# A graph transformer on one core: a pick of rows serves eight batches instead of four

## The chip, the core and the metric

The kernel runs on one core of a Trainium2 chip. The core has a matrix engine (TensorE, PE in the profile; its weight loads are listed apart as PEld), a vector engine (VectorE, DVE), a scalar engine (ScalarE, ACT), a general engine (GpSimd, POOL), which here only issues indirect gathers, and SyncE (SP), which only issues transfers. Each works through its own list of instructions in order and waits for the others through semaphores. The metric is the time on the device of one execution, in microseconds (us), the median of several runs.

## The reference

Three layers of a graph transformer run over 6,250 nodes with 64 features and 206,250 edges, sorted by target node; then a log-softmax, a residual and a normalization. One layer, shortened:

```python
q = x @ Wq + bq
k = x @ Wk + bk
v = x @ Wv + bv
e = edge_attr @ We
kj = k[src] + e
alpha = jnp.sum(q[dst] * kj, axis=-1) / jnp.sqrt(jnp.float32(D))
amax = jax.ops.segment_max(alpha, dst, num_segments=N)
p = jnp.exp(alpha - amax[dst])
denom = jax.ops.segment_sum(p, dst, num_segments=N)
w = p / denom[dst]
msg = (v[src] + e) * w[:, None]
agg = jax.ops.segment_sum(msg, dst, num_segments=N)
return agg + x @ Ws + bs
```

What matters here is `x[src]`: every edge needs the 64 features of its source node, and the sources are random.

## The kernel before

**Batches and steps.** The edges lie in 403 chunks of 512, four chunks to a batch (`LB`), so 100 full batches and a remainder. A layer runs over the batches in 99 steps (variable `u`) and some steps written out at its end. The nodes are 49 blocks of 128.

**Picked and gathered rows.** In layer 0 every chunk from batch 8 (`U0`) on is sorted on the chip by source: 22 windows (`WINDOWS`) of 16 slots (`SL`), where window w holds edges whose source lies in blocks 2w to 2w+3. Rows of edges with a slot need no gather. They are *picked*: for a pair of windows q, a one-hot matrix says which node of a block each slot wants (`hot`, built on VectorE from the `key` of each slot, in `aim`), and TensorE multiplies node rows (`halves`, split in three bf16 parts so that their sum is exact) by it: four blocks, three parts, two windows, 24 products (L1374 in `bank`). ScalarE copies the result from the accumulator `ps_x` into a ring, `kept` (L1383, L1386). Layer 0 has 8 such pairs, layers 1 and 2 have 11 (`PAIRS`). Edges without a slot are fetched by indirect DMA on GpSimd (L601), in layers 1 and 2 five transfers a batch, each let go by a small copy on ScalarE (`gate`, L635).

**Turns.** One pick serves four batches (`TURN`): 4 batches x 4 chunks x 16 slots = 256 columns. The pair q is picked at batches k with q % 4 = k % 4, so that in layers 1 and 2 three, three, three and two picks fall to successive steps, 283 picks a layer counting those cut at the layer's ends. The ring `kept` holds four batches. At step u the picks due at u+2 are made; by then step u has turned batch u+1 from the ring into rows (`naturals`).

**A step of layers 1 and 2** is, on TensorE: the scores of the last unit (L1673, L1678), the turning of the next batch from the ring (L1399, L1404), one pick (the *first place*), a transpose of gathered rows (L1650), the transposes of the probabilities (L1704), the other picks that are due (the *second place*), and the sums (L1717). VectorE reduces the scores (L1685), ScalarE takes the exponentials (L1692) and VectorE copies the transposed probabilities (L1707) in between. Work on finished groups of nodes (`finish`, `project`) is spread over the steps (`close_up`). There are two sets of four one-hot tiles; the next set is built as soon as a pick has been issued, in the buffers of that pick.

**Keys.** In layer 0 the `index` function of the sort writes each batch's keys to DRAM (`keyS`), in an order in which a pick's four batches lie side by side, in one or two transfers from ScalarE's queue; `load` reads a pick's keys with one transfer on SP that repeats them on all 128 partitions (L1307). Up to 7 key tiles wait in layers 1 and 2, and 3 in layer 0.

**The sort in layer 0.** `ranking` counts, for a set of chunks, the edges of each bin, one bin after the other. For each: a product of TensorE, a ScalarE pass that adds the carried count (`order`, L932), and a one-column VectorE operation that takes the new carried count `served` (L935) from its result, then a pause (`yield`) and two VectorE passes (L939, L940). `Move.across` turns sorted features and stores them through one buffer, `eN` (L1104).

**Boundaries.** Step 0 of layers 1 and 2 needs all eleven pairs picked for the first batches; this is done as far as possible while the last node groups of the layer before are finished (`early`), and the rest after them.

Of the kernel before, what the change touches and what calls it, by code (L numbers as in the profile page):

```python
# [39 lines left out]
KEYED = 12  # L40
PART = SLOTS - 2 * P
REST = P - PART
TURN = 4
GC = 16
# [398 lines left out]
def main_path(  # L443
# [80 lines left out]
    picks = ctx.enter_context(tc.tile_pool(name="picks", bufs=3))  # L524
# [8 lines left out]
    sorts = first_layer.enter_context(tc.tile_pool(name="sorts", bufs=2))  # L533

# [18 lines left out]
    keyS = dram.tile([KEYED, NT // TURN + 1, TURN, LB, 2 * SL], FP16, name="keyS")  # L553
# [317 lines left out]
    kept = {0: const.tile([P, TURN * LB, P], F32, name="kept0")}  # L871
    keys = const.tile([LB, KEYED, 2 * SL], FP16, name="keys")
# [20 lines left out]
    def ranking(i):  # L893
# [31 lines left out]
        for h in range(WINDOWS + 1):  # L925
# [7 lines left out]
            if h < WINDOWS:  # L933
                kinds = kinds_of(h + 1)
            nc.vector.tensor_scalar(  # L935
                served[:n, h + 1 : h + 2], order[:, CH - 1 :], float(SL * min(h + 1, WINDOWS) - 1), None, ALU.min
            )
            yield
# [72 lines left out]
    class Move:  # L1011
# [86 lines left out]
        def across(self, i):  # L1098
# [4 lines left out]
            eN = sorts.tile([P, 2 * T * D], F32, name="eN", bufs=1)  # L1103
# [5 lines left out]
        def index(self):  # L1109
# [16 lines left out]
            key = keys  # L1126
            order = key.rearrange("c (b a) (w e) -> c w a b e", b=TURN, w=2)
            for w in range(2):
                nc.vector.tensor_copy(
                    order[:, w, : FULL // TURN],  # L1130
                    pk[:, w * P : (w + 1) * P].rearrange("c (a b e) -> c a b e", b=TURN, e=SL),
                )
            tail = pk[:, 2 * P :].rearrange("c (h e) -> c h e", e=SL)
            nc.scalar.copy(order[:, :, 2, 2], tail[:, 2:4])
            for w in range(2):
                nc.scalar.copy(order[:, w, 2, :2], tail[:, 4 * w : 4 * w + 2])  # L1136
# [143 lines left out]
    class Picker:  # L1280


        def __init__(self, layer):
            self.layer = layer
            low = 0 if layer else U0
            self.jobs = []
            for k in range(low - TURN + 1, NT):
                for q in range(PAIRS[layer]):
                    if q % TURN == k % TURN:
                        self.jobs.append((k, max(k, low), min(k + TURN, NT), q))  # L1290
            self.loads, self.aims = list(self.jobs), list(self.jobs)
            self.keys, self.hots = {}, {}
            self.aimed = 0

        def load(self):

            while self.loads and len(self.keys) < (7 if self.layer else 3):
# [3 lines left out]
                shape = [P, TURN * LB * 2 * SL]  # L1301
                if self.layer:
                    key = later.tile(shape, FP16, name="key", bufs=7)
                else:
                    key = picks.tile(shape, FP16, name="key", bufs=3)
                a, b = self.span(job)
                nc.sync.dma_start(  # L1307
                    key[:, a * 2 * SL : b * 2 * SL],
                    keyS[q % TURN * KEYED // TURN + q // TURN, (job[0] + TURN) // TURN, a // LB : b // LB].rearrange("r c e -> (r c e)").partition_broadcast(P),
                )  # L1310
# [3 lines left out]
        def span(self, job):  # L1314

            _, k0, k1, _ = job
            return (0, TURN * LB) if k1 - k0 == TURN else (k0 % TURN * LB, ((k1 - 1) % TURN + 1) * LB)

        def aim(self):
# [23 lines left out]
        def due(self, k):  # L1343

            if not self.jobs or self.jobs[0][0] > k:
                return False
# [9 lines left out]
        def bank(self, k, tag="x"):  # L1356
# [7 lines left out]
            made = self.hots.pop(job)  # L1364
            q = job[3]
# [702 lines left out]
```

## Time and profile before

| what | value |
|---|---|
| median of three runs | 4270.91 us (4266.38 to 4275.15) |
| the profiled execution, its own time | 4275.86 us |
| the profiled execution, first to last instruction (span) | 4274.1 us |
| granted TensorE clock, mean | 0.948 |
| layer 0, steps | to about 1935 us |
| layer 1, steps | about 2056 to 3060 us |
| layer 2, steps | about 3180 to 4190 us |

The profile is one execution as the hardware recorded it. A row of a view gives source line, engine, operation, what is written and read (`out<-in`), the shape, a count, the busy time, the mean time of one in ns, and the engine's idle time just before such instructions with what ended it. Records of neighbouring products overlap, so the time a product costs is read from the starts of groups. "issue" means that the engine waited for nothing that the profile shows. The line numbers are those of the kernel before.

### The profile page before, as it was taken

What the parts mean: (1) busy time and instruction counts of PE and PEld (TensorE: products, weight loads), DVE (VectorE), ACT (ScalarE), POOL (GpSimd) and SP (SyncE); (2) the same over time, 40 slices, a digit from 0 to 9 for tenths busy, and PEclk for the clock granted to TensorE, in tenths of its full rate; (3) what the DMA queues carried; (4) which work ended last, traced back from release to release, by engine and by line L of the source; (5) the groups of instructions that cost most, each with busy time, mean ns of one, the idle gap of its engine ahead of it and who ended that gap; (6) DMA issues with size and microseconds to landing.
All of it is one profiled execution on the core that took longest, in us unless ns stands there. A gap on an engine that the chain in (4) does not pass through costs nothing.

```text
span 4274.1 us, 125157 instructions
## 1 busy us (share of the span) xinstructions
PE 3681.7 (86%) x44542; PEld 2464.7 (58%) x44542; DVE 2891.1 (68%) x9241; ACT 2394.9 (56%) x7113; POOL 2067.3 (48%) x1910
## 2 busy tenths in 40 slices
PE   4679998889999999987889999998778998888885
PEld 2345555555555655654666666666456666666663
DVE  5566888787788777774566666666456666666664
ACT  2334555555555555543566666666536676666664
POOL 4454554555455665552444444444415444444442
PEclk9789999999999999997999999999879999999997
DMA  5447787787777888874677777777647777777773
GB/s 119 101 131 188 201 213 203 192 211 200 206 198 211 226 212 209 218 196 131 146 183 189 192 185 186 188 193 182 152 96 191 177 181 184 187 186 179 176 187 83
DMA packets 828647, 768.02 MB, mean 180 GB/s; under 512 B 393233, under 2 KB 628903, under 8 KB 828014
## 3 DMA queue, kind: packets, MB, share of 16 engines
q1 hardware_dynamic: 673282, 571.05, 54.2%
q10 hardware_dynamic: 93932, 126.48, 8.4%
q0 software_dynamic: 60800, 62.38, 7.8%
q8 instruction: 356, 5.83, 0.6%
q14 instruction: 277, 2.27, 0.2%
HBM read 599.30 MB, written 160.27 MB: 178 GB/s over the span
## 4 chain that ended last, share of the span: by engine, by line


## 5 line engine op out<-in xcount | busy, mean ns | idle before, releaser
L601 POOL DMA_INDIRECT feat<-in_x,gate x860 | 1050.6, 1222 | 884.4 <-ACT gate L635 686.4
L1331 DVE TENSOR_SCALAR hot<-key,rank 128x512 bf16<-128x512 f16 (+3 forms) x3024 | 908.2, 350 | 372.5 <-PE ps_x L1374 167.5
L601 POOL DMA_INDIRECT feat<-x,gate x816 | 796.8, 976 | 745.3 <-ACT gate L635 479.1
L1374 PEld LDWEIGHTS <-halves 128*64 128x64 bf16 x18144 | 963.4, 113 | 285.7 <-issue 206.1
L1374 PE MATMUL ps_x<-hot,halves 128*64 128x256 bf16 (+1 forms) x13248 | 836.7, 276 | 41.6 <-issue 31.2
L1717 PE MATMUL ps_g<-feat,probT 128*32 128x128 f32 x9672 | 436.5, 283 | 92.4 <-issue 61.6
L1064 PE MATMUL ps_x<-hit,rest 128*64 128x512 bf16 (+3 forms) x3200 | 459.1, 359 | 6.0 <-issue 5.1
L1409 ACT COPY featT<-kept 64x512 f32<-64x512 f32 x584 | 361.5, 619 | 144.3 <-PE ps_g L1374 42.6
L1053 DVE TENSOR_SCALAR hit<-ruler,pos 128x512 bf16<-128x512 f16 (+3 forms) x1600 | 422.9, 334 | 1.7 <-PE ps_m L1078 1.4
L1717 PEld LDWEIGHTS ps_g<-feat,probT 128*32 128x32 f32 x9672 | 286.5, 112 | 221.5 <-issue 175.6
L1685 DVE TENSOR_REDUCE most<-ps_s 128x1 f32<-128x512 f32 x297 | 204.1, 687 | 300.6 <-PE ps_s L1678 111.9
L601 POOL DMA_INDIRECT few<-x,gate x198 | 193.6, 978 | 379.4 <-ACT gate L635 113.0
L1374 PE MATMUL ps_g<-hot,halves 128*64 128x256 bf16 (+2 forms) x4560 | 302.3, 281 | 74.1 <-ACT kept L1383 28.5
L1653 ACT COPY featT<-ps_a 64x512 f32<-64x512 f32 x584 | 338.6, 580 | 15.6 <-PE ps_a L1650 4.1
L1678 PE MATMUL ps_s<-featT,q 128*32 128x512 f32 x2376 | 333.7, 621 | 2.9 <-ACT featT L1653 1.3
L1064 PE MATMUL ps_x<-hit,raw 128*64 128x512 bf16 (+3 forms) x1600 | 311.0, 367 | 4.5 <-issue 4.1
L1383 ACT COPY kept<-ps_x 128x256 f32<-128x256 f32 (+2 forms) x502 | 185.1, 370 | 210.8 <-remote 128.6
L635 ACT COPY gate<-src_b 128x1 int32<-128x1 int32 x1762 | 289.9, 191 | 8.7 <-ACT keys L1136 1.4
L1692 ACT ACTIVATE prob<-ps_s,part 128x512 f32<-128x512 f32 x297 | 204.2, 688 | 161.0 <-issue 48.7
L1704 PE MATMUL ps_p<-ident,prob 128*128 128x128 f32 (+1 forms) x1224 | 199.1, 286 | 91.9 <-ACT prob L1692 89.8
L1064 PEld LDWEIGHTS <-rest 128*64 128x64 bf16 x3200 | 203.8, 113 | 116.6 <-issue 30.0
L1725 ACT COPY part<-ps_g 128x128 f32<-128x128 f32 (+1 forms) x309 | 82.2, 266 | 273.0 <-PE ps_g L1717 43.8
(261 smaller groups left out, 5162.4 us busy)
## 6 DMA issues: line engine op xcount, KB each, us to landing
feat<-eaP SPq DMA_DIRECT2D x292, 512.0 KB
featT<-eaS SPq DMA_DIRECT2D x292, 512.0 KB
key<-keyS SPq DMA_DIRECT2D x712, 128.0 KB
raw<-in_ea SPq DMA_DIRECT2D x200, 256.0 KB
eaS<-eT ACTq DMA_DIRECT2D x200, 256.0 KB
eaP<-eN ACTq DMA_DIRECT2D x200, 256.0 KB
to<-toS SPq DMA_DIRECT2D x292, 128.0 KB
part<-part SPq DMA_DIRECT2D x600, 32.5 KB
```

Of the source, the lines that this page charges most:

```text
L601: nc.gpsimd.indirect_dma_start(out=spares[layer, k] if c is None else loaded[layer, k][:, c, t, 0], out_offset=None, in_=xts[layer][:, :], ...
L635: copy(gate, index[:, i : i + 1])
L1053: nc.vector.tensor_scalar(hit, ruler[:, : REACH[t]], self.pos[:, at : at + 1], None, ALU.is_equal)
L1064: nc.tensor.matmul(self.px[i][j * D : (j + 1) * D, : REACH[t]], self.part(i, part)[:, (j * T + t) * D : (j * T + t + 1) * D], self.hits[t, ...
L1331: nc.vector.tensor_scalar(hot[:, a:b].rearrange("p k w e -> p (k w e)"), self.keys[job][:, a * 2 * SL : b * 2 * SL], rank[:, h : h + 1], None,
L1374: nc.tensor.matmul(px[w * D : (w + 1) * D, a:b], third(halves[block >= EARLY][:, at : at + 1], part)[:, 0], made[h][:, a:b, w], start=(h = ...
L1409: nc.scalar.copy(featT[:D, :, w * P : (w + 1) * P], kept[0][w * D : (w + 1) * D, at : at + LB])
L1653: nc.scalar.copy(self.featT[:D, :, at : at + P], pt[h * D : (h + 1) * D])
L1678: nc.tensor.matmul(self.p_s[rows], self.q[:, j * STRIDE : j * STRIDE + W], self.featT[:, j, :], start=False, stop=True)
L1685: nc.vector.tensor_reduce(top[:n], self.p_s[:n], AX.X, ALU.max)
L1692: nc.scalar.activation(self.prob[:n], self.p_s[:n], AF.Exp, bias=self.part[:n, P : P + 1], accum_out=self.part[:n, P + 1 : P + 2],)
L1717: nc.tensor.matmul(p_g[rows, :].rearrange("n (h d) -> n h d", h=2), self.probT[:, t, rows], batch[:, c + j, t], start=(t == 0), stop=(t == ...
```

## The change

One pick of layers 1 and 2 serves eight batches: 512 columns to a product, and the pair q is picked at batches with q % 8 = k % 8. Pairs 0 and 8, 1 and 9, 2 and 10 fall together, so successive steps have 2, 2, 2, 1, 1, 1, 1, 1 picks, 148 a layer. Where one pick is due its 24 products are divided: the first 12 in the first place (`open`), the others and the copy in the second (`shut`). The ring holds eight batches in layers 1 and 2; the one of layer 0 is a tile of its own. Both sets of one-hots stand in one pool, with two times four tiles of twice the size; 5 key tiles of twice the size take the place of 7. Layer 0 keeps turns of four.

The keys in DRAM are ordered by pair and batch. A batch's keys are written with one transfer; a pick whose first batch isn't at the start of the ring reads its keys with two. In the sort, the carried count `served` is taken after the pause, and `across` has two buffers.

```diff
 TURN = 4
+TURNS = (TURN, 8, 8)
...
-    keyS = dram.tile([KEYED, NT // TURN + 1, TURN, LB, 2 * SL], FP16, name="keyS")
+    keyS = dram.tile([WINDOWS // 2, NT, LB, 2 * SL], FP16, name="keyS")
...
             if h < WINDOWS:
                 kinds = kinds_of(h + 1)
+            yield
             nc.vector.tensor_scalar(
                 served[:n, h + 1 : h + 2], order[:, CH - 1 :], float(SL * min(h + 1, WINDOWS) - 1), None, ALU.min
             )
-            yield
...
-            eN = sorts.tile([P, 2 * T * D], F32, name="eN", bufs=1)
+            eN = sorts.tile([P, 2 * T * D], F32, name="natural", bufs=2)
...
-            r = k % TURN
-            for phases, job in ((slice(0, r + 1), k // TURN + 1), (slice(r + 1, TURN), k // TURN)):
-                if phases.start < phases.stop:
-                    those = slice(phases.start * KEYED // TURN, phases.stop * KEYED // TURN)
-                    nc.scalar.dma_start(keyS[those, job, r].rearrange("q c e -> c q e"), key[:, those])
+            nc.scalar.dma_start(keyS[:, k].rearrange("q c e -> c q e"), keys)
...
-            while self.loads and len(self.keys) < (7 if self.layer else 3):
+            while self.loads and len(self.keys) < (5 if self.layer else 3):
...
+                at = k0 % self.turn
+                m = min(k1 - k0, self.turn - at)
+                if at + k1 - k0 > self.turn > k1 - k0:
+                    nc.vector.memset(key[:, (k1 - k0 - m) * unit : at * unit], 0.0)
+                for there, a, b in ((at, k0, k0 + m), (0, k0 + m, k1)):
+                    if a < b:
+                        nc.sync.dma_start(
+                            key[:, there * unit : (there + b - a) * unit],
+                            keyS[q, a:b].rearrange("r c e -> (r c e)").partition_broadcast(P),
+                        )
...
-            pool = later if self.layer and self.aimed % 2 else picks
-            self.aimed += 1
+            pool, sets = (later, 2) if self.layer else (picks, 1)
             made = []
             for h in range(BW):
-                hot = pool.tile([P, TURN * LB, 2, SL], BF16, name="hot", bufs=BW)
+                hot = pool.tile([P, self.turn * LB, 2, SL], BF16, name="hot", bufs=BW * sets)
...
-        def bank(self, k, tag="x"):
+        def open(self, k, tag="x"):
...
+            px = ps(tag)[:, : self.turn * LB * SL].rearrange("p (k e) -> p k e", e=SL)
+            self.begun = job, self.hots.pop(job), px
+            self.products(range(BW // 2))
...
+        def shut(self):
+
+            if not self.begun:
+                return
+            self.products(range(BW // 2, BW))
+            job, _, px = self.begun
+            self.begun = None
...
+        def bank(self, k, tag="x"):
+
+            self.open(k, tag)
+            self.shut()
...
-                picker.bank(u + 2)
+                if picker.due(u + 2, 1):
+                    picker.bank(u + 2)
+                else:
+                    picker.open(u + 2)
...
                 close_up(3) if close else step()
+                picker.shut()
                 while picker.due(u + 2):
                     picker.bank(u + 2)
```

The order of the instructions, at three places. First VectorE in the middle of layer 1, one three-pick step before. `most` reduces the scores, `feat` are rows turned from the ring, `hot x4` is one set of one-hots for one pick, `probT` the probabilities that the sums wait for:

```order
L1685 TENSOR_REDUCE most<-ps_s 128x1
L1687 TENSOR_SCALAR part<-most 128x1
L1400 COPY feat<-ps_m 128x4x128
L1406 COPY feat<-ps_a 64x4x64
L1331 TENSOR_SCALAR hot<-key,rank 128x512 x4
L1707 COPY probT<-ps_p 128x512
L1331 TENSOR_SCALAR hot<-key,rank 128x512 x8
```

And now, in a step with one pick:

```order
L1705 TENSOR_REDUCE most<-ps_s 128x1
L1707 TENSOR_SCALAR part<-most 128x1
L1420 COPY feat<-ps_m 128x4x128
L1426 COPY feat<-ps_a 64x4x64
L1727 COPY probT<-ps_p 128x512
L1332 TENSOR_SCALAR hot<-key,rank 128x1024 x4
```

Three sets of one-hots for 256 columns were one set ahead of `probT` and two behind it; now one set of twice the size stands behind it (a two-pick step has one ahead of it and one behind it).

Second SP in the middle of layer 1, before, from a key load of the first place to the load of a batch's edge features for the sums (`eaP`). `to`, `q` and `featT` are the next unit's:

```order
L1307 DMA key<-keyS 128x512
L1598 DMA to_212<-toS 128x512
L1603 TENSOR_LOAD base
L1612 REGISTER_ALU
L1612 DMA q<-qq 128x80
L1629 DMA featT<-eaS 64x4x512
L1307 DMA key<-keyS 128x512 x2
L568 DMA feat<-eaP 128x1024
```

And now, in a step with one pick:

```order
L1618 DMA to_211<-toS 128x512
L1623 TENSOR_LOAD base
L1632 REGISTER_ALU
L1632 DMA q<-qq 128x80
L1649 DMA featT<-eaS 64x4x512
L1308 DMA key<-keyS 128x640
L1308 DMA key<-keyS 128x384
L568 DMA feat<-eaP 128x1024
```

The load ahead of `to` is gone from such a step, and the two behind `featT` are the two parts of one pick's keys.

Third VectorE in layer 0, a pass of the ranking, before. `kinds` marks the next bin, `served` is the carried count, `src_b` and `keys` belong to the sorted batch before:

```order
L920 TENSOR_SCALAR kinds<-half 128x4x96
L935 TENSOR_SCALAR served<-order 96x1 [waits Activation_49]
L1123 TENSOR_SCALAR src_b<-ps_a 128x9 [waits PE_49]
L1129 CAST keys<-ps_a 4x2x4x16 [waits DMAHW4_49,DMAHW3_49]
L1129 CAST keys<-ps_a 4x2x4x16
L939 SCALAR_TENSOR_TENSOR order<-bins,order 96x512 [waits DVE_49]
```

And now:

```order
L920 TENSOR_SCALAR kinds<-half 128x4x96
L1123 TENSOR_SCALAR src_b<-ps_a 128x9 [waits PE_49]
L1127 CAST keys<-ps_a 4x8x16 [waits DMAHW2_49]
L1127 CAST keys<-ps_a 4x8x16
L936 TENSOR_SCALAR served<-order 96x1 [waits Activation_49]
L939 SCALAR_TENSOR_TENSOR order<-bins,order 96x512 [waits DVE_49]
```

`served`, which waits for ScalarE, has moved behind what the pause lets in: the indices and keys of the batch sorted before.

More of the change, by code (lines that the diff above doesn't have):

```diff
@@ L1341, in aim, with due @@
             self.load()
-        def due(self, k):
-            if not self.jobs or self.jobs[0][0] > k:
+        def due(self, k, behind=0):
+            if len(self.jobs) <= behind or self.jobs[behind][0] > k:
                 return False
@@ L1395, in naturals @@
             featT = room_for(self.layer, k * LB)
[L1396 removed]
+            at = k % self.turn * LB
             pn = ps(tags[0])
```

53 lines of the change are left out of this document (24 added, 29 removed).

## The prediction

> **What bounds the kernel now.** I read the page's busy shares first, then the busy time by stage, then TensorE's timeline inside layer 1, then its groups of instructions in the same stages.
>
> ```profile
> span 4274.1 us, 125157 instructions
> PE 3681.7 (86%) x44542; PEld 2464.7 (58%) x44542; DVE 2891.1 (68%) x9241; ACT 2394.9 (56%) x7113; POOL 2067.3 (48%) x1910
> ```
>
> The stages of layer 0, layer 1 and layer 2 (from:to, length, busy us of PE, PEld, DVE, ACT and POOL, granted clock, DMA share, GB/s):
>
> ```profile
> 500.00:1300.00 800.00, 726.27 (x8457) 460.38 (x8456) 642.05 (x2171) 427.26 (x1241) 432.03 (x358) 0.97 0.77 204
> ...
> 2060.00:3040.00 980.00, 892.31 (x11830) 628.96 (x11826) 633.10 (x1850) 639.47 (x1951) 463.82 (x477) 0.99 0.75 186
> 3180.00:4190.00 1010.00, 897.77 (x11932) 632.62 (x11931) 644.79 (x1931) 676.86 (x2020) 477.92 (x487) 0.98 0.75 182
> ```
>
> In all three TensorE is busy about 90% of the time and the next engine 65 to 80%. So the change is worth what it takes off TensorE. Its timeline shows a two-pick step of layer 1 (2558.17 to 2565.88) and a three-pick step (2589.61 to 2599.09); L1673 begins a step:
>
> ```profile
> 2558.17 0.39 PE L1673 MATMUL ps_s<-to,codeT 128*128 128x512 bf16 x1
> ...
> 2560.51 1.50 PE L1374 MATMUL ps_x<-hot,halves 128*64 128x256 bf16 x24
> 2561.94 0.66 PE L1650 MATMUL ps_a<-ident,feat 128*128 128x128 f32 x4
> 2562.44 0.60 PE L1704 MATMUL ps_p<-ident,prob 128*128 128x128 f32 x4
> 2562.97 1.50 PE L1374 MATMUL ps_x<-hot,halves 128*64 128x256 bf16 x24
> 2564.41 1.08 PE L1717 MATMUL ps_g<-feat,probT 128*32 128x128 f32 x32
> 2565.42 0.63 PE L1434 MATMUL ps_a<-ident,rows_now 128*64 128x128 f32 x4
> 2565.88 0.38 PE L1673 MATMUL ps_s<-to,codeT 128*128 128x512 bf16 x1
> ...
> 2589.61 0.39 PE L1673 MATMUL ps_s<-to,codeT 128*128 128x512 bf16 x1
> ...
> 2594.40 2.81 PE L1374 MATMUL ps_x<-hot,halves 128*64 128x256 bf16 x48
> 2597.15 1.05 PE L1717 MATMUL ps_g<-feat,probT 128*32 128x128 f32 x20
> 2598.48 0.67 PE L1717 MATMUL ps_g<-feat,probT 128*32 128x128 f32 x12 [0.28 <-issue]
> 2599.09 0.39 PE L1673 MATMUL ps_s<-to,codeT 128*128 128x512 bf16 x1
> ```
>
> The two-pick step takes 7.71 us; without the 0.46 of L1434, which is a node group's work, 7.25. A second pick in the second place adds 2.75 - 1.44 = 1.31 (start to start), so a three-pick step should take 8.56. It takes 9.48. The 0.93 more stand in the sums (L1717): 1.01 us after 24 products, 1.94 after 48, in pieces, with idle that waits for nothing the profile shows. That holds over the whole stages (first row layer 1, second layer 2; last figures the idle before them):
>
> ```profile
> L1717 PE MATMUL ps_g<-feat,probT 128*32 128x128 f32 x3008 | 146.2, 277 | 35.3 <-issue 32.0 <-DVE probT L1707 1.9
> ...
> L1717 PE MATMUL ps_g<-feat,probT 128*32 128x128 f32 x3072 | 143.7, 277 | 27.8 <-issue 22.2 <-DVE probT L1707 3.6
> ```
>
> 3008 records are 94 steps: (146.2 + 35.3)/94 = 1.93 us a step, where the clean group above is 1.08 long. Layer 2: (143.7 + 27.8)/96 = 1.79. The excess is 80 + 68 = 148 us. I read it as instructions coming late: 48 products with their 48 weight loads are issued in 2.75 us, one per 29 ns, and the sums then want 64 in 1.01 us, one per 16 ns. After 24 products a reserve still covers that; after 48 it is used up.
>
> **The change, part by part.** All against the profiled execution's 4275.9 us; the three runs' median is 4270.9.
>
> *Products.* A layer's picks go from 283 to 148, with the same columns. The trace of before has no 512-column pick, but layer 0 streams 512 columns in the same paired form:
>
> ```profile
> 1955.05 0.60 PE L1064 MATMUL ps_x<-hit,rest 128*64 128x512 bf16 x4
> 1955.48 0.38 PE L1064 MATMUL ps_x<-hit,raw 128*64 128x512 bf16 x2
> 1955.69 0.60 PE L1064 MATMUL ps_x<-hit,rest 128*64 128x512 bf16 x4
> 1956.12 0.36 PE L1064 MATMUL ps_x<-hit,raw 128*64 128x456 bf16 x2
> ```
>
> Ten products in 1.07 us, 107 ns each; 24 are 2.57, and with the start of a group some 2.7, against 2.75 for 48 of 256. At 0.05 x 135 merged picks x 2 layers that is 13 us; between 0 and 30, I take 10. The array was streaming already.
>
> The Trainium skill's page "TensorE: Matmul & The Clock Gate", section "Wait — 56ns, not 53.3ns?", says so as a rule: warm products start N/2.4 GHz plus about 2.5 ns apart, so doubling N saves one 2.5 ns per merged pair. The rows agree (57 ns a product at 256, 107 at 512, in pairs). By that rule alone the products' term would be some 8 us, and the change would end near no change, which is the first rival.
>
> *The sums behind them.* In the changed order the second place holds 24 products of 512 columns (three steps of eight) or 12 (five of eight), never 48. That is at most one instruction per 54 ns, half today's rate, for as long. I expect sums of about 1.1 to 1.3 us everywhere, as after 24 products now. Not all of the 148 is due to the 48s, some belongs to waits for copies; I take 80%: -118, bounds 0 and -148.
>
> *Waits inside the picks.* The same view of L1374:
>
> ```profile
> L1374 PE MATMUL ps_x<-hot,halves 128*64 128x256 bf16 x6176 | 388.2, 274 | 15.5 <-issue 12.9 <-ACT kept L1383 1.0
> ...
> L1374 PE MATMUL ps_x<-hot,halves 128*64 128x256 bf16 x6192 | 400.5, 279 | 20.9 <-issue 16.1 <-ACT kept L1383 3.3
> L1704 PE MATMUL ps_p<-ident,prob 128*128 128x128 f32 x384 | 61.3, 283 | 42.3 <-ACT prob L1692 41.0 <-issue 0.4
> ```
>
> At 1.50 us for a group of 24 and 2.81 for one of 48 (the second place of three steps in four), the clean sum over 94 and 96 steps is about 375 and 382 us; the rows give 404 and 421. The third pick must wait for one-hots that DVE can only build once the first pick has freed their buffers. Now a step's two picks always have their two sets built a step ahead. I take half, -30 (0 to -65). L1704 waits 42 us in layer 2 for the exponentials; the first place is 1.3 us longer in three steps of eight and covers part: -10 (0 to -25).
>
> *DVE, ACT, key loads.* A one-hot of twice the size costs, by the forms 128x512 (354 ns) and 128x128 (260), 354 + 512 x 0.245 = 479 ns, at most 708:
>
> ```profile
> L1331 DVE TENSOR_SCALAR hot<-key,rank 128x512 bf16<-128x512 f16 x2848 | 867.6, 354 | 333.6 <-PE ps_x L1374 164.4 <-remote 84.9 <-PE ps_p L1704 23.5
> ...
> L1331 DVE TENSOR_SCALAR hot<-key,rank 128x128 bf16<-128x128 f16 x56 | 11.4, 260 | 19.0 <-DMA key<-keyS 15.3 <-remote 2.2 <-PE ps_x L1374 0.6
> ```
>
> That relieves DVE by over 100 us a layer, and the copies into the ring, half as many, relieve ACT; neither ends the step, so I count nothing. The one new wait, the copy of a pick begun early, ends at the second place as today's last copy does; behind it on ACT stand gate copies for gathers that run batches ahead. Key bytes are the same. Nine of eleven windows now take two loads each, so SP issues about as many as before.
>
> *The layer boundaries.* Before step 0 of layers 1 and 2 all eleven windows are picked for the first batches: 27 batch-picks with a turn of four, 47 with eight. 24 products of 256 columns are 1.31 us for four batches, 0.33 each: 20 x 0.33 = 6.6 us at either boundary. The last of these run with nothing else to do:
>
> ```profile
> 2035.28 3.79 PE L1374 MATMUL ps_x<-hot,halves 128*64 128x192 bf16 x48
> 2039.35 0.81 PE L1374 MATMUL ps_x<-hot,halves 128*64 128x256 bf16 x11 [0.29 <-issue]
> ...
> 2043.89 0.66 PE L1399 MATMUL ps_m<-ident,kept 128*128 128x128 f32 x4
> ```
>
> Part falls into earlier idle: +12 in all (0 to +20).
>
> *Layer 0.* DVE no longer stands at the count of one half while ACT finishes it, and ACT no longer waits for one buffer to be stored (350 to 1930 us; total, times, longest):
>
> ```profile
> DVE served L935 <- ACT order L932: 64.1, 28, 5.2
> ...
> ACT eN L1104 <- DMA eaP<-eN: 35.7, 23, 4.3
> ...
> PE ps_g L1374 <- DVE hot L1331: 11.4, 14, 1.9
> ```
>
> But TensorE itself waits little for DVE there; I take -12 (0 to -40). Against it, three quarters of layer 0's 190 picks take a second key load on SP, where two took this long, ahead of the next unit's loads:
>
> ```profile
> 1008.79 3.17 SPq L1307 DMA_DIRECT2D key<-keyS  x2
> 1012.05 0.41 SPq L1598 DMA_DIRECT2D to<-toS  x1
> ```
>
> Some 140 more issues of up to 1.6 us on a queue with slack until the next step: +5 (0 to +40).
>
> **Sum:** -10 - 118 - 30 - 10 + 12 - 12 + 5 = -163. One term is left: five steps in a row now hold one wide pick each. They want 7.2 us of TensorE, but today's mean step moves its data at 0.75 of 980/94 = 10.4, so 7.8 us of all DMA engines. The three long steps (8.56 + 1.3, about 9.9) can give it back, if loads run far enough ahead; +5 (0 to +60). That is -158 on 4275.9: 4118, and 4113 beside the median of the runs. I say **4115**.
>
> **Rivals.**
>
> *Nothing moves (0.09), 4266.* The sums' stall is not due to the rate of instructions but to what those steps do at that moment, and comes back behind 24 wide products. Then only products, boundaries and layer 0 are left: -10 + 12 - 12 + 5 = -5. For it: the idle has no named cause. Against it: the same sums after 24 products are whole.
>
> *Half of it (0.15), 4190.* The stall goes from the five short steps but stays behind 24 wide products: 3/8 of the steps at today's excess instead of 3/4, so -59 instead of -118, and half of the waits inside the picks stay with it: -10 - 59 - 15 - 10 + 12 - 12 + 5 + 5 = -84 on 4275.9, some 4190 beside the median.
>
> *The short steps do not get short (0.08), 4315, slower.* If the loads hold a short step at today's mean of 10.4 us, the long ones at 9.9 plus today's other waits, 10.9, the mean is (5 x 10.4 + 3 x 10.9)/8 = 10.6: +0.2 x 198 steps, +12 at the boundaries, -7 in layer 0, 45 on the median. It turns at a short step of about 10.1. Against it: the two-pick step above, the same TensorE work, took 7.7.
>
> **How the numbers follow.** The forecast, 0.68, spans by itself 4045 to 4200. The range takes in the half case and the lower part of nothing moves: 4045 to 4235; it leaves out the slower case, part of the second and a tail of larger gains. This kernel's measurement tells about 0.2% from no change, 4262 to 4279. Faster: 0.68 + 0.15 + 0.02 of the first rival, 0.85. Same: 0.07, the rest of that rival. Slower: the last one, 0.08.
>
> **What would show it.** The sums' group in the two stages at 1.1 to 1.3 us a step with little issue idle: the main step right; near 1.9: wrong. Products of 512 columns at 107 ns each. Short steps of 7.2 to 8.5 us, long ones of 10 to 11, a DMA share near 0.85. First scores of layers 1 and 2 some 5 us later after the last node group. Layer 0 within 20 us of before. What would make me wrong is a share of DMA near 1 in the short steps, or TensorE waiting there for keys or one-hots.

## The result, and the profile after the change

The changed kernel takes 4257.4 us (median of 20 runs, 4229.7 to 4269.0), the kernel before 4276.2 in the same series: a ratio of 0.9946, 95% interval 0.9929 to 0.9962. The forecast was 4115 with a range from 4045 to 4235, so the gain is about an eighth of the one forecast. The profiled run has a span of 4267.2 us. From the first and last scores of each layer's full batches (L1673 before, L1693 now), layer 0 ends at 1963 us instead of 1976, layer 1 lasts 1053 instead of 1044, layer 2 1044 instead of 1053, and the two boundaries are 5 us longer together. The two layers with the new picks cancel out in sum.

The busy time by stage of the changed kernel (columns as in the prediction):

```profile
500.00:1300.00 800.00, 727.16 (x8519) 460.58 (x8520) 651.31 (x2185) 430.85 (x1249) 494.20 (x360) 0.98 0.78 205
2060.00:3040.00 980.00, 881.25 (x8693) 472.87 (x8682) 546.82 (x1327) 612.02 (x1797) 477.94 (x470) 0.94 0.73 182
3180.00:4190.00 1010.00, 879.18 (x8819) 465.43 (x8815) 559.45 (x1415) 657.21 (x1888) 496.97 (x489) 0.95 0.73 181
```

A quarter of TensorE's instructions is gone, DVE and ACT have less to do, the DMA share is lower, and as many steps fit in as before. One column has moved the wrong way: the granted clock, from 0.99 and 0.98 to 0.94 and 0.95. TensorE's groups in layer 1 (2060 to 3040 us) show what went and what came:

```profile
L1379 PE MATMUL ps_x<-hot,halves 128*64 128x512 bf16 (+1 forms) x3079 | 375.5, 386 | 1.4 <-issue 1.3
L1698 PE MATMUL ps_s<-featT,q 128*32 128x512 f32 x752 | 123.6, 689 | 0.5 <-issue 0.3
L1737 PE MATMUL ps_g<-feat,probT 128*32 128x128 f32 x3004 | 105.9, 281 | 7.5 <-DVE probT L1727 6.5 <-issue 0.8
...
L1724 PE MATMUL ps_p<-ident,prob 128*128 128x128 f32 x376 | 59.0, 280 | 26.3 <-ACT prob L1712 26.0
...
L1466 PE MATMUL ps_g<-ws,xT 64*128 64x65 f32 x80 | 15.2, 347 | 32.9 <-ACT part L1745 30.6 <-issue 2.3
L1552 PE MATMUL ps_g<-ve,wT 128*128 128x64 f32 x80 | 14.5, 339 | 20.6 <-ACT part L1745 20.2 <-issue 0.4
```

And in layer 2 (3180 to 4190 us):

```profile
L1379 PE MATMUL ps_x<-hot,halves 128*64 128x512 bf16 (+3 forms) x3190 | 393.9, 388 | 4.6 <-issue 4.4
...
L1737 PE MATMUL ps_g<-feat,probT 128*32 128x128 f32 x3072 | 110.7, 287 | 5.4 <-DVE probT L1727 5.4
...
L1724 PE MATMUL ps_p<-ident,prob 128*128 128x128 f32 x388 | 66.5, 297 | 83.8 <-ACT prob L1712 82.7 <-issue 0.5
...
L1552 PE MATMUL ps_g<-ve,wT 128*128 128x64 f32 x88 | 14.8, 321 | 20.8 <-ACT part L1745 14.9 <-issue 5.9
```

The same lines of the kernel before in layer 1, as far as the prediction does not show them (L1678 is now L1698, L1704 L1724, L1532 L1552, L1446 L1466):

```profile
L1678 PE MATMUL ps_s<-featT,q 128*32 128x512 f32 x752 | 104.7, 619 | 0.7 <-ACT featT L1653 0.4
...
L1704 PE MATMUL ps_p<-ident,prob 128*128 128x128 f32 x380 | 58.9, 277 | 14.6 <-ACT prob L1692 13.8 <-issue 0.3
...
L1532 PE MATMUL ps_g<-ve,wT 128*128 128x64 f32 x80 | 11.9, 296 | 7.7 <-ACT part L1725 7.7
...
L1446 PE MATMUL ps_g<-ws,xT 64*128 64x65 f32 x80 | 11.1, 279 | 7.2 <-ACT part L1725 7.2
```

The sums (L1737) lost their stall as forecast: busy and idle went from 353.0 us in both layers to 105.9 + 7.5 + 110.7 + 5.4 = 229.5. The picks went from at least 825 to 775. That is some 173 us off TensorE's own line. Most of it came back as waits for results that follow from TensorE's own earlier ones: the transposes of the probabilities (L1724) wait 26 us for 15 in layer 1 and 84 for 42 in layer 2, the node groups' products (L1466, L1552) 54 for 15 in layer 1. It came back, too, as slower work: the same scores (L1698) take 123.6 us for 104.7 in layer 1.

The products themselves cost what was forecast: in layer 1, pairs of 512 columns start 216 ns apart, 108 ns a product. But the steps did not follow. Those with one pick take 10.1 and 10.0 us on average in layers 1 and 2, where 7.2 to 8.5 was foreseen (the shortest takes 7.2), and those with two take 11.5 and 11.4.

**A step seen closely.** TensorE tells the other engines that a result is ready by incrementing a semaphore; I call such an increment a completion. The changed kernel's timeline (start, us, engine, what):

```profile
2639.73 1.08 PE L1737 MATMUL ps_g<-feat,probT 128*32 128x128 f32 x32
...
2642.49 0.95 POOL L601 DMA_INDIRECT feat<-x,gate  x1 [2.12 <-ACT feat L618]
...
2643.74 0.95 POOL L601 DMA_INDIRECT feat<-x,gate  x1 [0.30 <-issue]
...
2644.95 0.66 PE L1670 MATMUL ps_a<-ident,feat 128*128 128x128 f32 x4
2644.99 0.94 POOL L601 DMA_INDIRECT feat<-x,gate  x1 [0.30 <-issue]
...
2645.44 0.60 PE L1724 MATMUL ps_p<-ident,prob 128*128 128x128 f32 x4
...
2645.97 1.49 PE L1379 MATMUL ps_x<-hot,halves 128*64 128x512 bf16 x12
2646.24 0.95 POOL L601 DMA_INDIRECT few<-x,gate  x1 [0.30 <-issue]
...
2647.49 0.95 POOL L601 DMA_INDIRECT feat<-x,gate  x1 [0.30 <-issue]
2649.79 1.18 ACT L1673 COPY featT<-ps_a 64x512 f32<-64x512 f32 x2 [3.32 <-remote]
2649.85 0.69 DVE L1727 COPY probT<-ps_p 128x512 f32<-128x512 f32 x1 [5.26 <-remote]
...
2650.60 1.93 PE L1737 MATMUL ps_g<-feat,probT 128*32 128x128 f32 x32 [3.14 <-DVE probT L1727]
```

TensorE's transposes L1670 and L1724 are over at 2646.0. ACT and DVE, who copy their results and have nothing else to do, start at 2649.8. In the trace's semaphore events TensorE's last completion before that arrives at 2643.18. The next eight, those of these transposes among them, arrive within 0.35 us, at 2649.63 to 2649.98; the record that sent the oldest of them had ended over 4 us earlier. Between 2642.5 and 2648.4 GpSimd issues five gathers with 0.3 us between them. Then follows a second loss (windows of the same run; the column before the DMA share is the granted clock):

```profile
2647.30:2650.70 3.40, 0.26 (x6) 0.10 (x8) 0.85 (x2) 0.89 (x2) 0.95 (x1) 0.95 0.79 183
2650.70:2657.50 6.80, 6.80 (x48) 2.72 (x49) 1.92 (x5) 3.05 (x11) 3.11 (x3) 0.53 0.49 123
2660.90:2667.80 6.90, 3.96 (x55) 2.37 (x55) 2.36 (x6) 3.08 (x11) 4.15 (x4) 0.97 0.74 168
```

After 3.4 us in which TensorE all but stood still, its clock is half for 6.8 us. So the sums at 2650.60 take 1.93 us for the 1.08 at 2639.73.

Is that the rule? I counted TensorE's completions, and the matmul records that send one (by their ends), by the time since the last gather began, in the stretches 2060 to 3040 us and 500 to 1300 us on chip A, 1900 to 2700 and 500 to 1300 on chip B:

```
completions per us (records that send one, per us), by us since a gather began
kernel, stretch     chip  0-0.4      0.4-0.8    0.8-1.2    1.2-1.6    1.6-2.0    2.0-2.4
before, layer 1     A     1.0 (2.0)  0.8 (2.1)  0.5 (2.1)  2.3 (1.8)  4.3 (1.9)  3.2 (2.3)
after,  layer 1     A     0.7 (1.5)  0.6 (1.3)  0.4 (1.5)  1.4 (1.5)  4.2 (1.9)  2.6 (1.8)
before, layer 0     A     1.0 (2.1)  0.9 (2.2)  0.7 (2.1)  2.0 (2.0)  5.1 (2.2)  5.4 (2.3)
wide_b, layer 1     B     1.6 (1.6)  2.3 (2.4)  1.2 (1.2)  1.5 (1.6)  1.7 (1.8)  2.0 (1.8)
turn4,  layer 1     B     2.2 (2.6)  2.0 (2.2)  2.1 (2.1)  2.1 (2.1)  2.6 (2.5)  2.5 (2.6)
turn4,  layer 0     B     2.5 (2.6)  2.0 (2.1)  2.2 (2.3)  2.6 (2.7)  1.6 (1.6)  2.1 (2.0)
```

On chip A, where the result was measured, TensorE works evenly and its completions reach the others in bursts: few during the first 1.2 us after a gather's start, about twice as many as are sent once it is over. B stands for other chips, of which the experiments tell (`wide_b` is the changed kernel there); on them completions arrive as they are sent. Not every completion has a record: in layer 1, 1679 of 2029 on A before the change and 1207 of 1444 after it, and 1320 of 1346 on B in `wide_b`. So the low rates on A are somewhat too low, but records that are missing can't make the bursts.

So the theory: **on this chip a gather holds TensorE's completions up.** A step issues five gathers of 0.95 us with 0.3 behind each, 6.3 us in all, and has a row of hops from TensorE to another engine and back (scores to exponentials, transposes to copies, sums to the next use of their bank). I put the rest of the 10.4 us of a step to these hops, without adding them up, with TensorE's work beside both. The stall in the sums is part of it: of the 235 gaps of over 0.2 us between starts inside the sums of both stages before the change (120 us), two thirds end within 0.04 us of a completion's arrival, where 5% of random moments in these gaps lie so near to one. My reading is that TensorE had run ahead as far as it may with completions outstanding, and that fewer instructions stop it later while the others still wait; the trace shows only that the gaps and the hold-up end together. The rivals: the steps are held by their bytes (loads), or by the array's own work.

### The profile page after: what moved, and what is told of

Its sections match the earlier page's. It is cut to its first block, busy times and chain, and to the rows that moved or that the text cites. A ratio compares the mean times of both kernels' runs of the same rounds, so it can differ in the third digit from the quotient of the medians.

```text
span 4267.2 us, 109959 instructions
## 1 busy us (share of the span) xinstructions
PE 3637.8 (85%) x38062; PEld 2119.3 (50%) x38062; DVE 2726.8 (64%) x8167; ACT 2354.4 (55%) x6819; POOL 2170.9 (51%) x1910
## 4 chain that ended last, share of the span: by engine, by line
## 5 line engine op out<-in xcount | busy, mean ns | idle before, releaser
L601 POOL DMA_INDIRECT feat<-in_x,gate x860 | 1116.4, 1298 | 806.8 <-ACT gate L635 610.1
L601 POOL DMA_INDIRECT feat<-x,gate x816 | 818.2, 1003 | 622.9 <-ACT gate L635 353.6
L1379 PEld LDWEIGHTS <-halves 128*64 128x64 bf16 x11664 | 624.0, 114 | 482.1 <-issue 203.3
L1332 DVE TENSOR_SCALAR hot<-key,rank 128x1024 bf16<-128x1024 f16 (+4 forms) x1944 | 724.0, 421 | 168.8 <-PE ps_x L1379 53.7
L1379 PE MATMUL ps_x<-hot,halves 128*64 128x512 bf16 (+2 forms) x6816 | 822.8, 384 | 10.4 <-issue 10.1
L601 POOL DMA_INDIRECT few<-x,gate x198 | 209.4, 1058 | 476.5 <-ACT gate L635 182.4
L1737 PE MATMUL ps_g<-feat,probT 128*32 128x128 f32 x9672 | 359.2, 286 | 35.4 <-DVE probT L1727 22.9
L1698 PE MATMUL ps_s<-featT,q 128*32 128x512 f32 x2376 | 361.8, 645 | 2.4 <-ACT featT L1673 0.9
L1673 ACT COPY featT<-ps_a 64x512 f32<-64x512 f32 x584 | 338.7, 580 | 35.2 <-PE ps_a L1670 13.7
L1737 PEld LDWEIGHTS ps_g<-feat,probT 128*32 128x32 f32 x9672 | 265.7, 114 | 153.2 <-issue 77.0
L1724 PE MATMUL ps_p<-ident,prob 128*128 128x128 f32 (+1 forms) x1224 | 205.7, 293 | 147.9 <-ACT prob L1712 145.8
L1064 PE MATMUL ps_x<-hit,raw 128*64 128x512 bf16 (+3 forms) x1600 | 308.1, 363 | 10.9 <-issue 10.6
L1727 DVE COPY probT<-ps_p 128x512 f32<-128x512 f32 x204 | 139.7, 685 | 231.1 <-PE ps_p L1724 172.0
```

The source lines that it names most:

```text
L601: nc.gpsimd.indirect_dma_start(out=spares[layer, k] if c is None else loaded[layer, k][:, c, t, 0], out_offset=None, in_=xts[layer][:, :], ...
L1064: nc.tensor.matmul(self.px[i][j * D : (j + 1) * D, : REACH[t]], self.part(i, part)[:, (j * T + t) * D : (j * T + t + 1) * D], self.hits[t, ...
L1332: nc.vector.tensor_scalar(hot[:, a:b].rearrange("p k w e -> p (k w e)"), self.keys[job][:, a * 2 * SL : b * 2 * SL], rank[:, h : h + 1], None,
L1379: nc.tensor.matmul(px[w * D : (w + 1) * D, a:b], third(halves[block >= EARLY][:, at : at + 1], part)[:, 0], made[h][:, a:b, w], start=(h = ...
L1673: nc.scalar.copy(self.featT[:D, :, at : at + P], pt[h * D : (h + 1) * D])
L1698: nc.tensor.matmul(self.p_s[rows], self.q[:, j * STRIDE : j * STRIDE + W], self.featT[:, j, :], start=False, stop=True)
```

## Experiments

The runs were made in four sets, each on a chip of its own with the kernel before beside it. In two sets (chips 14 and 4) that took 4314.1 and 4312.5 us, near the 4276.2 of the result; I call this kind of chip A. In the other two (chips 7 and 15) it took 3831.0 and 3830.4, a tenth less; I call this B. What sets the two kinds apart outside the kernel I don't know; no chip was used in two sets, so whether it stays with the chip isn't shown either. All times, with each layer from the first to the last scores of its full batches:

```
kernel          kind  time     ratio to before (95%)     layer 0 ends  layer 1  layer 2
wide            A     4293.2   0.9949 (0.9932 - 0.9966)  1984          1055     1044
turn4_c         A     4300.8   0.9972 (0.9953 - 0.9991)  1967          1055     1058
wide_more_b     A     4476.7   1.0379 (1.0352 - 1.0407)  1984          1154     1138
wide_third_c    A     4219.9   one run                   1964          1044     1031
wide_plain_b    A     4133.5   one run                   1988           964      951
narrow_plain_c  A     4244.0   one run                   2014          1018     1007
wide_b          B     3777.9   0.9850 (0.9819 - 0.9881)  1775           907      900
turn4           B     3823.5   0.9967 (0.9948 - 0.9985)  1776           913      918
turn4_b         B     3825.6   0.9989 (0.9977 - 1.0001)  1768           924      923
wide_more       B     3787.3   0.9869 (0.9836 - 0.9903)  1767           913      907
wide_third      B     3660.2   one run                   1772           860      847
wide_plain      B     3923.5   1.0235 (1.0207 - 1.0262)  1766           970      956
narrow_plain    B     4043.6   1.0561 (1.0522 - 1.0599)  1811          1014     1012
narrow_plain_b  B     4063.6   one run                   1830          1020     1010
```

### Without gathers on GpSimd

```
 def take(layer, k, c, t, index):
+    out = spares[layer, k] if c is None else loaded[layer, k][:, c, t, 0]
+    if layer:
+        at = k * P % (NB * P - P)
+        nc.sync.dma_start(out, xts[layer][at : at + P, :])
+        return
     nc.gpsimd.indirect_dma_start(
...
```

In the changed kernel:

> The changed kernel with the indirect gathers of layers 1 and 2 on GpSimd's queue turned into plain DMAs of as many rows and bytes on SP's queue (fixed rows, so what these layers compute is not the reference; times are read only). Theory (held-up signals): while GpSimd issues a gather, TensorE's completions reach the other engines late (in the trace 0.3 to 1.3 of them per us in the first 1.2 us after a gather's start, 4 to 6 per us at 1.6 to 2 us, with TensorE's own records even), so a step lasts about five gathers (1.25 us each) plus its hops from TensorE to the others, whatever TensorE's work is. Without gathers on GpSimd the steps fall from 10.45 to 8.2-9.2 us and the kernel to 3980-4130. Rival (loads): a step is held by its bytes; same bytes, so 4230-4290. Rival (array): TensorE's own work fills the step; same products, 4230-4290. SP has some five issues a step more in all of them, which could cost up to 1 us a step if SP ends steps; it is idle for half of the time now.

In the kernel before:

> The same replacement of gathers by plain DMAs in layers 1 and 2, in the kernel before the change (rows fixed, so these layers do not compute the reference). Theory (held-up signals): TensorE's own work at 48 narrow products behind each other keeps about 1 us a step of stall in the sums, so the gain is smaller than in the changed kernel: 4120-4230, and the distance between the two kernels grows from 19 us to 100-200. If the sums' stall is itself an effect of the gathers, it goes too, and the distance stays under 60. Rivals (loads, array): 4250-4300.

Both sets of numbers missed: they were meant for A, and this first set ran on B. 3924 and 4044 are below the ranges, and yet both are slower than the kernel before there. On B the completions are not held up (the table above), and the plain DMAs on SP's queue made these layers longer than the gathers had. The two kernels came out 120 us apart, as if the sums' stall had stayed, and yet it was gone: both branches of the second expectation were half wrong, and what else keeps the narrow version longer there was not tried. With B the theory had to name the place, and the same kernel was sent again:

> The changed kernel with plain DMAs on SP's queue for the gathers of layers 1 and 2, once more (these layers then do not compute the reference). On the faster chip it took 3922 us: 1766 to the end of layer 0, 970 and 956 from the first to the last scores of layers 1 and 2. Theory: on a chip where before takes 4276, layer 0, which keeps its gathers, ends at about 1960, and layers 1 and 2 take 955 to 990 as on the faster chip, since nothing holds the completions up there. Rival (the slower chip is slower in all): layers 1 and 2 also take a tenth longer, 1050 to 1070. On the faster chip: 3922 again.

It ran on A and took 4133, 160 us less than the changed kernel with its gathers there. The busy time of this run on A, in layer 0 and in layer 1:

```profile
500.00:1300.00 800.00, 722.28 (x8407) 456.61 (x8406) 643.68 (x2165) 427.57 (x1241) 491.83 (x355) 0.97 0.77 203
2150.00:2950.00 800.00, 723.17 (x7480) 395.56 (x7481) 481.10 (x1185) 531.97 (x1547) 0.00 (x0) 0.96 0.78 196
```

The same of the run on B (wide_plain):

```profile
500.00:1300.00 800.00, 769.89 (x9423) 493.24 (x9412) 715.11 (x2413) 476.17 (x1377) 534.43 (x400) 0.99 0.86 229
2000.00:2800.00 800.00, 718.34 (x7495) 395.99 (x7491) 473.93 (x1183) 531.89 (x1554) 0.00 (x0) 0.95 0.77 193
```

In layer 0, where the gathers stay, 800 us hold 355 gathers on A and 400 on B, and all engines do a tenth less on A. In layer 1, without them, the rows are the same: 7480 and 7495 matmuls, DMA share 0.78 and 0.77. Layers 1 and 2 take 964 and 951 us on A, 970 and 956 on B. So A is not slower as such; it is slower where GpSimd gathers. The rival "slower in all" (1050 to 1070) falls. As many bytes are moved and the products are the same, so neither loads nor the array's work held the steps on A. One thing more changed, which I did not separate: the plain DMAs read consecutive rows, the gathers random ones.

The kernel before without gathers was sent twice more, for A:

> The kernel before with plain DMAs on SP's queue for the gathers of layers 1 and 2 (these layers then do not compute the reference). On the faster chip layers 1 and 2 took 1014 and 1012 us from the first to the last scores. Theory: where before takes some 4300 they take that too, within 1.5%, and the idle that no record explains in front of the sums (32 and 22 us in the stages of layers 1 and 2 of the kernel before) is under 5 us there, as it is TensorE waiting for its own held-up completions. Rival (the prediction's reading: 48 narrow products use up the reserve of instructions): that idle stays at 20 us or more, with or without gathers.

> The kernel before with plain DMAs on SP's queue for the gathers of layers 1 and 2 (these layers then do not compute the reference), meant for a chip where before takes some 4300. Theory: layers 1 and 2 take 1000 to 1030 us each, as on the faster chip (1014 and 1012), though layer 0 ends some 200 us later than there, and the unexplained idle in front of the sums is under 5 us a stage. Rival (48 narrow products use up the reserve of instructions): that idle stays at 20 us or more.

The first fell on B again (1020 and 1010 us), the second on A: 1018 and 1007 us. Its groups in layer 1, the sums (now L1722) first:

```profile
L1722 PE MATMUL ps_g<-feat,probT 128*32 128x128 f32 x2955 | 102.0, 279 | 0.0
...
L1709 PE MATMUL ps_p<-ident,prob 128*128 128x128 f32 x369 | 60.8, 290 | 62.5 <-ACT prob L1697 62.5
```

The sums stand behind 48 narrow products as before the change, and their idle is 0.0. That speaks against the prediction's reading, too many instructions, on the same kind of chip. Alone it is not enough, as TensorE now waits 62.5 us at the transposes, in which instructions could catch up; `turn4` on B, below, has 48 narrow products and no stall at a TensorE that is busy for 96% of the time. Without gathers the wide picks are worth much: layers 1 and 2 together take 1915 us for 2025 on A (two chips), 1925 for 2026 on B (one set).

### One gather more

```
 nc.gpsimd.indirect_dma_start(
...
+if layer and c is None:
+    again = nodes.tile([P, D], F32, name="again", bufs=2)
+    nc.gpsimd.indirect_dma_start(
+        out=again,
...
```

> The changed kernel with one more gather for each unit of layers 1 and 2 on GpSimd: 128 rows, taken a second time into a tile that nobody reads (six gathers a unit for five). Theory (held-up signals): each gather adds 0.9 to 1.25 us to a step, as steps with more gathers are longer by now (0.95 us for one in a fit over the steps of the trace): +170 to +250 us, 4430-4510. Rivals (loads, array): GpSimd is idle for half of the time, and 32 KB more for a unit of 1.9 MB are 2%: 4250-4300.

> The changed kernel with one more gather for each unit of layers 1 and 2 once more, beside the changed kernel itself. Theory: where completions are held up during a gather (before at 4276), it is 170 to 250 us longer than the changed kernel; where they aren't (before at 3831), under 40 us longer, as GpSimd is idle for 45% of the time. Rivals (loads, array): under 40 us on both.

The first fell on B, so its numbers, meant for A, don't apply. It took 3787, against 3778 for the changed kernel there in another set: some 10 us, within the intervals. On A it took 4477 against 4293 in the same set: 184 us for 200 gathers, 0.92 us each, as the theory put it. The same instruction that costs next to nothing on B costs about its whole length on A. The gathers themselves take as long on both (463.82 us for 477 in layer 1 of before on A, 425.51 for 436 in `turn4` on B).

### The changed kernel, and narrow picks in it

The changed kernel itself was run in one set on each chip; `turn4` is the changed kernel with

```
-TURNS = (TURN, 8, 8)
+TURNS = (TURN, TURN, TURN)
```

> The changed kernel itself. The first four runs fell on a chip where the kernel before takes 3831 us, not 4276, and where TensorE's completions arrive evenly during gathers. Theory (held-up signals, as a property of the place the program runs in): on such a chip the change is worth what it takes off TensorE and its waits, 0.975 to 0.989 of before (3735 to 3790); on a chip where before takes about 4276, 0.993 to 0.996 again. Rival (the change is worth the same everywhere): 0.993 to 0.996 on both.

> The changed kernel itself once more, as a measure for the others of this call. Where before takes some 4300: 0.993 to 0.997 of it. Where before takes some 3830 (completions not held up): theory 0.975 to 0.989; rival (the change is worth the same everywhere) 0.993 to 0.997.

> The changed kernel with picks of four batches and 256 columns in layers 1 and 2 as before the change; what stays of the change is layer 0, the layout of the keys and five key buffers for seven. If, as the two traces have it, layer 0 gave 13 us and the wide picks nothing in sum: 4255-4275. If the wide picks gave the 19 us: 4270-4295.

> The changed kernel with picks of four batches and 256 columns again in layers 1 and 2, once more. On the faster chip it took 0.9967 of before. Where before takes some 4300, the theory (completions held up, step bound by gathers and hops) gives the wide picks nothing: within 0.3% of the changed kernel beside it, 0.993 to 0.998 of before, its gain being layer 0's. Rival (the wide picks bring the 0.5%): 0.998 to 1.002 of before. Where before takes some 3830: 0.9967 again, over 0.5% slower than the changed kernel beside it.

> The changed kernel with picks of four batches and 256 columns again in layers 1 and 2, meant for a chip where before takes some 4300. Theory (completions held up, step bound by gathers and hops): the wide picks are worth nothing there, so 0.992 to 0.997 of before, layer 0's gain alone, and layers 1 and 2 take 1040 to 1060 us each from the first to the last scores, as in the changed kernel. Rival (the wide picks bring the 0.5%): 0.998 to 1.002. Where before takes some 3830: 0.9967 to 1.0 again.

On A the change is 0.9949 again, on B 0.9850. The narrow version is 0.9972 on A and 0.9967 and 0.9989 on B; `turn4` fell on B, its numbers were meant for A. So the wide picks alone are worth some 1.2% on B (3778 against 3826 in one set) and 0.2% on A, where the intervals overlap. `turn4_c` does not decide between the theory and the rival there: 0.9972 lies just above the range of the one, and its interval takes in part of both. The sums of the narrow version in layer 1 on A (turn4_c):

```profile
L1737 PE MATMUL ps_g<-feat,probT 128*32 128x128 f32 x3008 | 144.1, 280 | 34.0 <-issue 29.6 <-DVE probT L1727 2.7
```

And on B (turn4):

```profile
L1737 PE MATMUL ps_g<-feat,probT 128*32 128x128 f32 x2784 | 94.0, 276 | 0.0
```

On A (144.1 + 34.0)/94 = 1.89 us a step, on B 94.0/87 = 1.08, with the same instructions. The stall that carried my forecast does not exist on B, so the number of instructions alone does not make it.

### A third of the products

```
-                for part in range(3):
+                for part in range(1 if self.layer else 3):
```

> The changed kernel with one of three products of each pick in layers 1 and 2 (8 for 24; the lower two parts of the picked rows are left out). That takes 16 x 107 ns = 1.7 us off TensorE for each of 148 picks a layer, 253 us a layer. Theory, where before takes some 4300: a step is bound by five gathers and the hops behind them, and less TensorE work turns into waiting: layers 1 and 2 get 20 to 90 us shorter each, the kernel 40 to 180. Rival (array, TensorE's work sets the step): 200 us or more a layer. Where before takes some 3830, TensorE is busy 96% of the time and the theory gives 130 to 250 a layer too.

> The changed kernel with one of three products of each pick in layers 1 and 2 (the lower two parts of the picked rows are left out), meant for a chip where before takes some 4300. On the faster chip it took 118 us off, not the 260 or more that I had expected. TensorE has 253 us a layer less to do. Theory (a step is five gathers and the hops behind them): 0 to 120 us in all, 4170 to 4290. Rival (TensorE's work sets the step): 300 us or more, under 3990.

On A, some 253 us less of TensorE's work a layer (an estimate, 148 picks of 16 products at 107 ns) made layer 1 11 us shorter and layer 2 13, the kernel 73 (against `wide` in another set; 28 of that at the boundaries, 20 by the end of layer 0, where the two kernels are the same). TensorE's work does not bound a step there. The busy time in the two layers on A:

```profile
2050.00:3050.00 1000.00, 757.68 (x6816) 400.40 (x6814) 548.43 (x1382) 627.06 (x1845) 491.34 (x484) 0.85 0.71 182
3160.00:4160.00 1000.00, 741.49 (x6763) 381.26 (x6766) 552.66 (x1431) 661.45 (x1905) 501.84 (x489) 0.85 0.73 183
```

TensorE is busy for 76% and 74%, the mean granted clock has fallen to 0.85, and the step is nearly as long as before. On B the layers got 47 and 53 us shorter, where I had expected 130 to 250: a miss. There the exponentials become the longest wait of TensorE, as its group of transposes in layer 1 (800 us) shows:

```profile
L1724 PE MATMUL ps_p<-ident,prob 128*128 128x128 f32 x376 | 63.0, 293 | 64.6 <-ACT prob L1712 64.4
```

What holds them on B was not tried.

## Why the prediction was wrong, by its own steps

- **"The change is worth what it takes off TensorE"**: this is the step that failed. A busy share of 90% was read as the bound. On A the steps are set by GpSimd's gathers and what waits behind them: a third of the products took 24 us off the two layers where the rival (the array's work) asked for 400 or more, one gather more per batch cost 0.92 us each, and without gathers the layers take as long as on B. TensorE's share is high in part because its waiting is counted in its records: the sums of the narrow version are busy for 144.1/94 = 1.53 us a step on A (`turn4_c`) and 1.08 on B (`turn4`).
- **"I read it as instructions coming late"**: wrong cause, right row. The stall did go (-123 us for -118), as I read it since half as many instructions stand behind one another unfinished, but on B it is absent with all of them (`turn4`): it was the hold-up showing in one of its places. The idle was put down to "issue", which names no cause, and I supplied one without a second reading to test it. Counting TensorE's completions by the time since a gather began was possible on the trace of before.
- **Products and waits inside the picks**: -50 at least, for -10 and -30. Right, and given back in the same way.
- **"L1704 waits ... -10"**: +53. A wide first place covers the exponentials' time only if the scores' completion comes in time; that it came late here is shown for the step above, not counted over the layers. This is the wait that took the stall's place in layer 2.
- **Boundaries** +5 for +12; **layer 0** -13 in the two traces for -7. On B, layer 0 ended at 1766 to 1776 in the kernels made from the changed one and at 1811 and 1830 in those made from the one before; on chip 4 of kind A it was 1964 and 1967 for 2014. So its part may be larger and something given back later (`turn4` gains 0.3% or less); five key buffers for seven were not tried apart.
- **The short steps** did not get short (10.1 and 10.0 us for 7.2 to 8.5), but they did not run into the loads: the DMA share fell to 0.73, where 0.85 was foreseen.
- **The rival "nothing moves"** gave 4266 and was near in time (0.9946 of 4276 is 4253), with a mechanism that did not happen: it had the stall stay in the sums. The rival "the short steps do not get short" had the steps nearly right (10.4 for 10.0, 10.9 for 11.4) and the time wrong (4315), since it put them to the loads and added them to the long steps' waits. No rival had anything but TensorE or the loads set the step.

The half clock is the second place to which time went. I divided the stages of layers 1 and 2 of four kernels on A (before, after, turn4_c, wide_third_c) into the windows of 3.41 us at whose borders the clock changes. Of 1668 windows at full clock with less than 0.9 us of TensorE idle (time in none of its matmul records), none is followed by a window at half clock; of 129 with 2 us or more, all are; of 125 with 1.3 to 2 us, 53. Before the change 17 windows of 581 ran at half clock, after it 62: some 150 us more, worth up to 75 of TensorE's work. The Trainium skill's page "TensorE: Matmul & The Clock Gate", section "What's actually happening", has a free-running window of 3413 ns, which the trace shows, and half clock after at least one idle window; here 2 us of one window were enough. The wide picks made that worse, as they gathered many small stalls into few long ones: TensorE's idle stretches of 2 us or more in these stages went from 9 (28 us) to 54 (146 us), those of 0.2 to 0.5 us from 243 to 54, and the narrow version `turn4_c` has 8 and 277.

What stays open: what in A makes a gather hold the completions up, whether it is GpSimd's issuing or the reading of random rows, and whether it is the signal or the last stage of the work that is late. The traces show the arrival alone.

## What to carry to other kernels

A busy share near 90% says that an engine is seldom empty, not that it bounds: before counting on less work for it, look at how long after its instructions their results are taken up by engines that have nothing else to do, and at what else runs in that time. Where idle is put down to no cause, make a second reading of the trace that could refute the cause you have in mind. And measure on more than one chip before sizing a gain: this change is worth 1.5% on one kind and 0.5% on the other.

## What the runs showed of the hardware that was not expected

- On the chips of kind A, and not on those of kind B, TensorE's completions reach the other engines late while GpSimd issues an indirect DMA: 0.4 to 1.0 of them per us in the first 1.2 us, 4.2 to 5.1 per us at 1.6 to 2.0. One gather more per batch then cost 0.92 us of the kernel's time each; the kernel before takes 4276 to 4314 us there for 3831.
- After 2 us or more without matmuls in a 3.41 us window, TensorE's clock was half in the next window in 129 of 129 cases.
- Plain DMAs of 128 consecutive rows of 256 bytes on SP's queue in place of gathers of random rows on GpSimd's made layers 1 and 2 longer on B (970 and 956 us for 907 and 900, in two sets).
